# Two fused convolution layers: attention products paired in PSUM banks of their own, the limit on a softmax sum on GpSimd, the large quotients behind the small one

## The chip, the cores and the metric

The kernel runs on one core of a Trainium2 chip. The metric is the device time of one execution in microseconds; less is better. TensorE is called PE in the profile (PEld is its weight load), VectorE DVE, ScalarE ACT, GpSimd POOL, and SyncE, which issues most DMAs, SP.

## The reference, cut to what matters

```python
x = x + layer0(_gn(x), ...)   # 8 images of 256 channels, 64 x 64, all in float32
x = x + layer1(_gn(x), ...)

# layer 0, an involution
x1, x2, x3 = conv1x1(x, w1), conv1x1(x, w2), conv1x1(x, w3)     # 32, 32, 256 channels
h = relu(bn(concat([x1, unfold3(reflect_pad(x2))])))            # 32 * 10 channels
w = conv1x1(relu(bn(conv1x1(h, cw1))), cw2, cb2)                # 32 groups x 9 taps
out = sum_k unfold3(zero_pad(x3))[g, s, k] * w[g, k]            # g: 32 groups, s: 8

# layer 1, attention over 7 x 7 windows beside a dynamic convolution
att = softmax(q . (unfold7(k) + unfold7(pe)))                   # 4 heads of 64 channels, 49 keys
out_att = att . unfold7(v)
wts = softmax(conv1x1(x, Wfc).reshape(C, 9), over the 9)
hid = relu(dwconv(x, w1)); oc = dwconv(hid, w2)
out_conv = sum_9(oc * wts)                                      # = oc * sum(wts), as oc is the same for all 9
return rate1 * out_att + rate2 * out_conv
```

The kernel writes the last sum as a quotient: with eight exponentials taken relative to the ninth, the sum of the eight is `tot`, and the weight is tot / (tot + 1).

## The kernel before, in words

Each image is cut into 8 bands of 8 rows (512 positions). One loop runs over `g`, the bands of all images, starting 12 bands early: `g` is the band that layer 1 works on, and layer 0 works 10 to 12 bands ahead of it in the same loop. The first 12 rounds (`g < 0`, "alone") have layer 0 only; the last ones have layer 1 only. A round has 8 steps `s`: two channel halves `ct` of four steps `m`, and each step takes two 8 x 8 tiles of queries of the band.

The order of every engine's instructions is written out by hand (`tc.manual_schedule`): `advance()` moves a counter on, six times in a step, and `after(n, f)` puts work n moves later. Work with a place in the step goes into the lists `mid` and `end`, which `beside` fills. What an engine does is then in program order; the framework adds the semaphores, also for the rotation of buffers: a tile tag with n buffers hands them out in turn, and writing into a buffer waits for the last reader of the tile that had it n tiles ago.

What a step of layer 1 does, with the lines of the profile:

- PE: weighted values of an earlier step, 64 columns of the array wide (L747, 16 records, since a float32 product makes two); scores of this step, 64 x 64 (L703, 8); transposes of the last step's probabilities into `ptp` (L735, 4); the first `pf`, a 128 x 512 product for the dynamic weights (L825, 4); one product of the kind that the step has in `mid` (queries `pq` L637, keys `pk` L658, values `pv` L563, layer 0's `p3` L369, value transposes `pvt` L607); the second `pf`.
- DVE: masks the scores and takes their maximum (L712), adds weighted values to the output tile `xr` (L757), runs four taps of the depthwise convolutions (L782 and L808), takes the small reciprocal of the softmax sums (L727).
- ACT: exponentials of the scores (L720), scaling by the reciprocal (L729), copies `ptp` to `pt` (L737), exponentials of `pf` into `ex` (L830), and empties the other PSUM tiles.
- POOL: adds the `ex` of this step to that of the step before (L1026).

After the fourth step of a half, `dynamic_sum` adds the two halves of `ex` on POOL (L838); DVE adds 1 and limits (L845) and takes the quotient in two pieces, called large reciprocals below (L846, L850); POOL multiplies twice and adds to `xr` (L855, L856, L857, called the weighing below); SP stores `xr` (L862) after the second half.

Beside that runs layer 0 for later bands: `small_maps` makes `p12` (L328), from which ACT writes `x2` in eight pieces (L343, L347); `hidden_maps` scales it (L418) and makes `ph` (L429) and `h2n` (L435); `tap_weights` makes the nine taps' weights, three to a PSUM tile `pw` (L447), DVE multiplies each with the values (`prod`, L460, two buffers), POOL adds each product to `xg` (L468), and SP stores the result (L500).

[...] Before, `gen`, a tag of five, serves `ptp`, `pf`, `p12`, `ph`, `pw` and all `mid` products; the scores' tile `sco` takes two, and the weighted values lie in its free columns; `acc` of the depthwise convolutions takes one.

In SBUF, `ex` has three buffers, one for each step, and `rec`, the large reciprocal, one of its own. The end of `dynamic_sum`, which the change leaves as it is, and the lines that take an `ex` tile and free the one before:

```python
def weigh():
    engine.tensor_mul(tot, tot, rec)              # L855: tot is ex[:, 1] of the half's last step
    engine.tensor_mul(oc, oc, tot)                # L856: the last reader of that ex tile
    engine.tensor_add(xr[:, ct], xr[:, ct], oc)   # L857
    if ct == NCT - 1:
        after(6, store)
...
ex, exb = w1.tile([P, 2, BAND], F32, tag="ex", name=f"ex_{nm}", bufs=3), ex if m else None
branch_weights(b, i, ct, m, 0, ex)                # the first pf, L825, and its exponential, L830
...
after(4, lambda ex=ex, exb=exb: nc.gpsimd.tensor_add(ex, ex, exb))   # L1026, where there is an exb
```

Of the kernel before, what the change touches and what calls it, by code (L numbers as in the profile page):

```python
# [10 lines left out]
F32 = mybir.dt.float32  # L11
# [7 lines left out]
P = 128  # L19
# [20 lines left out]
TG = 3  # L40
# [25 lines left out]
TAPS_AT = (1, 3, 5), (0, 2, 4)  # L66
PRODUCTS_AT = ((1, 2, 7), (1, 2, 5), (1, 2, 7)), ((7, 14, 10), (9, 17, 13), (12, 20, 16))
# [19 lines left out]
def conv_layers_kernel(ctx: ExitStack, tc: tile.TileContext, ins: dict, out: bass.AP):  # L87
# [98 lines left out]
    def layer1_loads():  # L186


        last = w1.tile([P, NCT, 1, C], F32, tag="rec", name="last", bufs=1)
# [35 lines left out]
    def gn_affine(sts, means, name, done):  # L225
# [9 lines left out]
        def group_means(v, k):  # L235
            pg = ps.tile([P, n], F32, name=f"pg_{name}_{k}", tag="gen", bufs=5)
            nc.tensor.matmul(pg, means, v, start=True, stop=True)
            return pg
# [49 lines left out]
    def scaled_weights(b):  # L288
# [3 lines left out]
        def scale(sc, bi):  # L292
            im.w12s = w0.tile([P, NCT, 2 * REL], F32, tag="w12s", name=f"w12s_{b}", bufs=1)
            im.w3s = w0.tile([P, NCT, C], F32, tag="w3s", name=f"w3s_{b}", bufs=1)
            for kt in range(NCT):
                nc.vector.tensor_scalar(im.w12s[:, kt], w12[:, kt], sc[:, kt : kt + 1], None, ALU.mult)
                nc.vector.tensor_scalar(im.w3s[:, kt], w3[:, kt], sc[:, kt : kt + 1], None, ALU.mult)
            after(5, lambda: through(bi))

        def through(bi):  # L300
            pb = ps.tile([P, 1 + NCT], F32, tag="gen", name=f"pb_{b}", bufs=5)
# [18 lines left out]
    def small_maps(b, i):  # L320
# [4 lines left out]
        p12 = ps.tile([P, R // 2, W], F32, tag="gen", name=f"p12_{b}_{i}", bufs=5)  # L325
# [36 lines left out]
    def value_maps(b, i, mt):  # L362
# [4 lines left out]
        p3 = ps.tile([P, BAND], F32, tag="gen", name=f"p3_{b}_{i}_{mt}", bufs=5)  # L367
# [41 lines left out]
    def hidden_maps(b, i, at):  # L409
# [5 lines left out]
        def hidden(t):  # L415
            n = P if t == 0 else 96
            hid = w0.tile([P, R, W], F32, tag="hid", name=f"hid_{b}_{i}_{t}", bufs=2)
# [5 lines left out]
        def conv(first, last):  # L423
            if first == 0:
                im.ph = ps.tile([P, SR, W], F32, tag="gen", name=f"ph_{b}_{i}", bufs=5)
            for t in range(first, last):
                n = P if t == 0 else 96
                for q in range(NQR):
                    nc.tensor.matmul(  # L429
                        im.ph[q * REL : (q + 1) * REL], c1[:n, t], hids[t][:n, q * SR : (q + 1) * SR],  # L430
                        start=(t == 0), stop=(t == 2),
                    )

        def relu():
            nc.scalar.activation(h2n[i % 2][:, :, :W], im.ph, AF.Relu, bias=bn2b, scale=bn2s)  # L435

        hidden(0)
        for n, f in zip(at, (lambda: hidden(1), lambda: conv(0, 2), lambda: hidden(2), lambda: conv(2, 3), relu)):
            after(n, f)

    def tap_weights(b, i, u, alone, at):
# [3 lines left out]
        pw = ps.tile([P, TG, SR * HP], F32, tag="gen", name=f"pw_{b}_{i}_{u}", bufs=5)  # L445
        for j in range(TG):
# [55 lines left out]
        for j, n in enumerate(at):  # L502
            after(n, lambda j=j: product(j))
# [626 lines left out]
```

## Time and profile before

| | us |
|---|---|
| median of three runs | 4154.88 (4153.21 to 4155.15) |
| the profiled execution | 4152.64 |
| its span, first to last instruction | 4150.9 |
| start of the first scores / of band 54's / last scores | 246.3 / 3611.8 / 4131.5 |
| granted clock, mean | 0.993 |

A line of the page's group list gives line, engine, operation, output and inputs, shapes and count, then busy us and the mean ns of one. A line of a timeline gives start and duration in us, then the same, and in brackets how long the engine had been idle and what ended that. In a PE row the duration includes the last record's modelled end, so the time that a group takes is read from start to start. The table by stage gives for each stretch its length, then the busy us and count of PE, PEld, DVE, ACT, POOL, the clock, the DMA share and GB/s.

### The profile page before, as it was taken

The page shows a single profiled execution, that of the slowest core. Times are in us where ns is not written, and L with a number is a line of the kernel's source. Part 1 is how long each engine was busy: PE and PEld are TensorE (multiplying, and loading weights), DVE is VectorE, ACT ScalarE, POOL GpSimd, SP SyncE. Part 2 cuts the span into 40 slices and gives each one's busy share as a digit, 9 for nine tenths or more (in the row PEclk, how much of TensorE's full clock was granted, in tenths as well). Part 3 has the DMA queues.
Part 4 walks back from the last instruction along what each step waited for, and adds up shares of the span by engine and source line. Part 5 has one row for each costly group of instructions (what it writes and reads, how often), then busy time and mean ns, then how long its engine had stood idle before and what let it go on. Part 6 is the DMA issues. An engine that isn't in the chain of part 4 may idle for free.

```text
span 4150.9 us, 72735 instructions
## 1 busy us (share of the span) xinstructions
PE 4022.6 (97%) x25292; PEld 2126.8 (51%) x25292; DVE 3591.9 (87%) x7248; ACT 3081.0 (74%) x7726; POOL 2923.0 (70%) x1902
## 2 busy tenths in 40 slices
PE   6789999999999999999999999999999999999998
PEld 3345555555555555555555555555555555455554
DVE  5878998899898898889998898888988889977777
ACT  3467778777787777877778777777778777687776
POOL 4767777677786777777777777777777677744554
PEclk8999999999999999999999999999999999999999
DMA  8854234234244233334234234244233233111100
GB/s 226 194 135 111 73 91 109 72 94 109 62 101 107 76 94 98 81 94 109 72 85 118 72 94 105 66 101 106 71 82 99 65 87 85 33 41 39 39 28 21
DMA packets 381264, 367.89 MB, mean 89 GB/s; under 512 B 55648, under 2 KB 282720, under 8 KB 380640
## 3 DMA queue, kind: packets, MB, share of 16 engines
q1 hardware_dynamic: 377568, 358.68, 34.3%
q8 instruction: 200, 3.28, 0.3%
q10 hardware_dynamic: 3328, 4.55, 0.3%
q14 instruction: 168, 1.38, 0.1%
HBM read 261.42 MB, written 101.71 MB: 87 GB/s over the span
## 4 chain that ended last, share of the span: by engine, by line
PE 71%; DVE 14%; POOL 6%; ACT 5%; DMA 2%; issue 2%; SPq 1%; POOLq 0%; ACTq 0%; DVEq 0%
PE pf L825 33%; PE ptp L735 5%; PE sco L747 5%; PE pk L658 5%; PE sco L703 5%; PE p L369 5%; DVE prod L460 4%; PE pq L637 4%; POOL xg L468 3%; PE pvt L607 2%; PE pv L563 2%; DVE acc L808 2%; PE pw L447 2%; DVE acc L782 2%; POOL ex L1026 2%
## 5 line engine op out<-in xcount | busy, mean ns | idle before, releaser
L825 PE MATMUL pf<-yp,c_wfc 128*128 128x512 f32 x4096 | 1930.5, 595 | 10.6 <-ACT vc L581 5.0
L468 POOL TENSOR_TENSOR xg<-xg,prod 128x1024 f32<-128x1024 f32 x549 | 1203.9, 2193 | 96.6 <-DVE prod L460 64.1
L825 PEld LDWEIGHTS pf<-yp,c_wfc 128*128 128x128 f32 x4096 | 729.9, 190 | 690.5 <-issue 619.4
L1026 POOL TENSOR_TENSOR ex<-ex,ex 128x1024 f32<-128x1024 f32 x384 | 907.7, 2364 | 61.9 <-ACT ex L830 57.2
L830 ACT ACTIVATE ex<-pf 128x512 f32<-128x512 f32 x1024 | 607.3, 593 | 297.9 <-POOL ex L1026 141.3
L782 DVE SCALAR_TENSOR_TENSOR acc<-yp,c_chan,acc 128x504 f32<-128x504 f32 (+3 forms) x1104 | 766.2, 694 | 42.3 <-ACT acc L773 21.7
L460 DVE SCALAR_TENSOR_TENSOR prod<-pw,c_par,x3q 128x1040 f32<-128x1040 f32 x576 | 733.9, 1281 | 66.8 <-PE pw L447 21.6
L808 DVE SCALAR_TENSOR_TENSOR acc<-hid,c_chan,acc 128x504 f32<-128x504 f32 (+3 forms) x1024 | 757.8, 740 | 20.2 <-ACT acc L802 2.1
L855 POOL TENSOR_TENSOR ex<-ex,rec 128x512 f32<-128x512 f32 x127 | 162.3, 1278 | 809.5 <-DVE rec L850 767.1
L729 ACT ACTIVATE prob<-prob,tot 128x196 f32<-128x196 f32 x1024 | 411.6, 450 | 387.2 <-DVE tot L727 386.4
L712 DVE CUSTOM_DVE_ANT_0 prob<-sco,c_mask 128x196 f32<-128x196 f32 x1024 | 325.5, 355 | 272.4 <-PE sco L703 272.0
L720 ACT ACTIVATE prob<-prob,nmax 128x196 f32<-128x196 f32 x1024 | 461.4, 454 | 46.9 <-DVE nmax L712 45.3
L747 PEld LDWEIGHTS sco<-pt,vt 112*64 112x64 f32 x8160 | 283.8, 137 | 182.3 <-issue 51.7
L737 ACT COPY pt<-ptp 112x512 f32<-112x512 f32 x511 | 297.0, 581 | 105.0 <-PE ptp L735 103.0
L735 PE MATMUL ptp<-ident,prob 128*112 128x128 f32 x2044 | 341.7, 287 | 31.2 <-ACT prob L729 30.5
L747 PE MATMUL sco<-pt,vt 112*64 112x64 f32 x8160 | 347.0, 227 | 0.0
L735 PEld LDWEIGHTS ptp<-ident,prob 128*112 128x112 f32 x2044 | 203.9, 133 | 201.4 <-issue 77.7
L703 PE MATMUL sco<-kb,qb 64*64 64x196 f32 x4096 | 295.2, 357 | 0.0
L563 PE MATMUL pv<-yp,c_wv 128*128 128x512 f32 (+2 forms) x576 | 247.3, 554 | 0.6
L369 PE MATMUL p<-xc,w3s 128*128 128x512 f32 x512 | 244.4, 601 | 0.0
L658 PE MATMUL pk<-yp,c_wk 128*128 128x512 f32 (+2 forms) x576 | 240.8, 545 | 0.0
L637 PE MATMUL pq<-yp,c_wq 128*128 128x512 f32 x512 | 240.6, 592 | 0.0
(140 smaller groups left out, 5294.0 us busy)
## 6 DMA issues: line engine op xcount, KB each, us to landing
x<-x3n SPq DMA_DIRECT2D x128, 264.0 KB, 2.1
x3q<-x SPq DMA_DIRECT2D x128, 264.0 KB, 7.2
xc<-in_x SPq DMA_DIRECT2D x64, 512.0 KB, 5.0
xg<-in_x SPq DMA_DIRECT2D x256, 128.0 KB, 4.8
x<-xg SPq DMA_DIRECT2D x256, 128.0 KB, 2.4
yp<-x SPq DMA_DIRECT2D x128, 256.0 KB, 3.3
xr<-x SPq DMA_DIRECT2D x64, 512.0 KB, 5.8
out_x<-xr SPq DMA_DIRECT2D x64, 512.0 KB, 3.1
```

The source lines that it names most:

```text
L369: nc.tensor.matmul(p3, im.w3s[:, kt, mt * P : (mt + 1) * P], im.xc[i][:, kt, :], start=(kt == 0), stop=(kt == NCT - 1),)
L460: nc.vector.scalar_tensor_tensor(prod[:, :, :RUN], pw[:, j, :RUN].unsqueeze(1).to_broadcast([P, SHARE, RUN]), par[:, PCB2 + k : PCB2 + k + 1],
L468: nc.gpsimd.tensor_add(im.xg[i], im.xg[i], rows(prod))
L703: nc.tensor.matmul(sco[half[t], h, :NKEY], qb[half[h], 2 * m + t].rearrange("p r c -> p (r c)"), kb[half[h], :, c0 : c0 + KW], start=True, ...
L720: nc.scalar.activation(prob[:, h, :NKEY], prob[:, h, :NKEY], AF.Exp, bias=nmax[:, h : h + 1], scale=-1.0, accum_out=tot[:, h : h + 1],)
L735: nc.tensor.transpose(ptp[:, h, ch], prob[:, h, ch * CHUNK : (ch + 1) * CHUNK], ident)
L747: nc.tensor.matmul(po[half[h], :, t * TQ : (t + 1) * TQ], im.vt[i + ch, m][:n, t, (2 * ct + h) * HD : (2 * ct + h + 1) * HD], pt[:n, h, ch ...
L782: nc.vector.scalar_tensor_tensor(o, yp[:, ct, ra + dr : rb + dr, ca + dc : cb + dc], chan[:, ct, CW1 + k : CW1 + k + 1], o, ALU.mult, ALU.add,
L808: nc.vector.scalar_tensor_tensor(o, hid[:, ra + dr : rb + dr, ca + dc : cb + dc], chan[:, ct, CW2 + k : CW2 + k + 1], o, ALU.mult, ALU.add,)
L825: nc.tensor.matmul(pf, wfc[:, kt, 2 * m + j, ct * P : (ct + 1) * P], images[b].yp[i][:, kt, PAD : PAD + R], start=(kt == 0), stop=(kt == N ...
L830: nc.scalar.activation(ex[:, j].rearrange("p (r c) -> p r c", r=R), pf, AF.Exp)
L1026: after(4, lambda ex=ex, exb=exb: nc.gpsimd.tensor_add(ex, ex, exb))
```

## The change

- Scores are computed for two steps at once, at even steps, into the two banks of `sco` (columns 0 to 195 and 196 to 391 of each); the masking of each step stays in its step, as `masked`.
- The weighted values of two steps are computed together behind them, in a bank of their own (`small`), which also takes `p12` and `ph` when they are due. `gen` goes from five banks to four.
- The transposes of an odd step's probabilities stand behind the weighted values of the next even step; those of an even step stand behind the first `pf` of the odd step.
- The three products of `ph` become one group at step 6, with three `hid` buffers for two.
- Taps are made two to a `pw` tile at steps 1 to 5 (before: three at steps 1, 3 and 5), and their products follow 1 and 2 moves later.
- `dynamic_sum`'s "add 1 and limit" moves from DVE to POOL, right behind L838; the large reciprocals are taken 7 and 2 moves later instead of 5 and 3, which puts the first behind the small reciprocal of its step; they go into the half of `ex` that is free by then.
- The scaling of layer 0's weights moves from DVE to ACT.

```diff
-TAPS_AT = (1, 3, 5), (0, 2, 4)
-PRODUCTS_AT = ((1, 2, 7), (1, 2, 5), (1, 2, 7)), ((7, 14, 10), (9, 17, 13), (12, 20, 16))
+TAPS_AT = (1, 2, 3, 4, 5), (0, 2, 4)
+PRODUCTS_AT = ((1, 2),) * 5, ((7, 14, 10), (9, 17, 13), (12, 20, 16))
...
-                nc.vector.tensor_scalar(im.w12s[:, kt], w12[:, kt], sc[:, kt : kt + 1], None, ALU.mult)
+                nc.scalar.activation(im.w12s[:, kt], w12[:, kt], AF.Copy, scale=sc[:, kt : kt + 1])
...
-        p12 = ps.tile([P, R // 2, W], F32, tag="gen", name=f"p12_{b}_{i}", bufs=5)
+        p12 = home[:, 2 * P :].rearrange("p (r c) -> p r c", r=R // 2)
...
+    def score_of(sco, h, m):
+        return sco[:, h, m % 2 * NKEY : (m % 2 + 1) * NKEY]
...
-        ptp = ps.tile([CHUNK, 2, 2, P], F32, tag="gen", name=f"ptp_{nm}", bufs=5)
+        ptp = ps.tile([CHUNK, 2, 2, P], F32, tag="gen", name=f"ptp_{nm}", bufs=4)
...
+    def small_tile(nm):
+        return ps.tile([P, 4 * P], F32, tag="small", name=f"small_{nm}")
+
+    def weigh_steps(steps, home):
+        po = home[:, : 2 * P].rearrange("p (s r c) -> p s r c", s=2, r=R)
+        return [(a, weighted_values(*a, pt, po)) for a, pt in steps]
...
         engine.tensor_add(tot, tot, ex[:, 0])
-        rec = w1.tile([P, BAND], F32, tag="rec", name=f"rec_{b}_{i}_{ct}", bufs=1)
+        engine.tensor_scalar(tot, tot, 1.0, 1.0e37, ALU.add, ALU.min)
+        rec = ex[:, 0]
         n = BAND // 2
         def quotient():
-            nc.vector.tensor_scalar(tot, tot, 1.0, 1.0e37, ALU.add, ALU.min)
             nc.vector.reciprocal(rec[:, :n], tot[:, :n])
-            after(3, second)
+            after(2, second)
...
-        after(5, quotient)
+        after(7, quotient)
...
                 if g >= 0:
-                    sco = score_tile(nm)
-                    weighted = [(a, weighted_values(*a, pt, sco)) for a, pt in pending]
-                    prob, nmax = scores(b, i, ct, m, sco)
+                    weighted = []
+                    if m % 2 == 0:
+                        sco = score_tile(nm)
+                        for e in range(2):
+                            scores(b, i, ct, m + e, sco)
+                        small = small_tile(nm)
+                        weighted, pending = weigh_steps(pending, small), []
+                        if s == 0 and g + AHEAD < B * NB:
+                            mid.append(small_maps(*divmod(g + AHEAD, NB), small))
+                        if s == 6 and convs:
+                            convs.pop()(small)
+                        if before is not None:
+                            pending.append((before[:-1], transposed(nm, before[-1])))
+                    prob, nmax = masked(nm, m, sco)
                     for a, po in weighted:
                         add_values(*a, po)
-                    pending = [] if before is None else [(before[:-1], transposed(nm, before[-1]))]
                     tot = exponentials(nm, prob, nmax)
                 advance()
                 if g >= 0:
                     branch_weights(b, i, ct, m, 0, ex)
+                    if m % 2:
+                        pending.append((before[:-1], transposed(nm, before[-1])))
```

## Prediction, made before the changed kernel ran

> **What bounds the kernel now.** I read the page first, then busy time by stage, then the timelines of PE, ACT and GpSimd (POOL) over one band in the middle. The page says PE:
>
> ```profile
> PE 4022.6 (97%) x25292; PEld 2126.8 (51%) x25292; DVE 3591.9 (87%) x7248; ACT 3081.0 (74%) x7726; POOL 2923.0 (70%) x1902
> ```
>
> By stage (columns: us, then PE, PEld, DVE, ACT, POOL busy) PE is at 98.8% between the ramp and the tail, DVE at 90%, POOL at 75%:
>
> ```profile
> 1000.00:1500.00 500.00, 494.17 (x3152) 263.36 (x3151) 448.78 (x907) 385.92 (x968) 374.15 (x243) 1.00 0.37 91
> ```
>
> So PE's own order is the first limit, and a shorter PE band is worth something only until another engine's order binds. PE timeline, start and us, of step 1 of a band, then its steps 6 and 7:
>
> ```profile
> 2004.92 1.88 PE L369 MATMUL p<-xc,w3s 128*128 128x512 f32 x4
> 2006.73 0.69 PE L747 MATMUL sco<-pt,vt 112*64 112x64 f32 x16
> 2007.34 0.58 PE L703 MATMUL sco<-kb,qb 64*64 64x196 f32 x8
> 2007.85 0.65 PE L735 MATMUL ptp<-ident,prob 128*112 128x128 f32 x4
> 2008.34 1.88 PE L825 MATMUL pf<-yp,c_wfc 128*128 128x512 f32 x4
> 2010.06 0.60 PE L607 MATMUL pvt<-ident,vc 128*112 128x128 f32 x4
> ...
> 2052.53 0.57 PE L703 MATMUL sco<-kb,qb 64*64 64x196 f32 x8
> 2053.44 0.78 PE L735 MATMUL ptp<-ident,prob 128*112 128x128 f32 x4 [0.34 <-ACT prob L729]
> 2054.36 1.98 PE L825 MATMUL pf<-yp,c_wfc 128*128 128x512 f32 x4
> ```
>
> Start to start, a full 128x512 pair takes 1.72 us, but 1.81 ahead of a change to 64-column tiles; the small groups take 0.61 (L747), 0.51 (L703) and 0.49 (L735). The last rows show PE waiting in step 7 for scaled probabilities (0.91 and 0.92 in place of 0.51 and 0.49; in step 6 it loses 0.23 more). This band starts at 1999.49 (L747 of step 0), the next at 2061.06: 61.57 us, 1.06 of it these waits.
>
> GpSimd in that band, with the ACT row that waits for it:
>
> ```profile
> 2015.70 1.28 POOL L855 TENSOR_TENSOR ex<-ex,rec 128x512 f32<-128x512 f32 x1 [6.11 <-DVE rec L850]
> ...
> 2039.39 2.17 POOL L468 TENSOR_TENSOR xg<-xg,prod 128x1024 f32<-128x1024 f32 x1
> ...
> 2042.40 1.04 POOL L621 TENSOR_TENSOR pe<-pecol,perow 128x512 f32<-128x512 f32 x1
> 2048.31 1.28 POOL L855 TENSOR_TENSOR ex<-ex,rec 128x512 f32<-128x512 f32 x1 [4.86 <-DVE rec L850]
> 2049.67 1.27 POOL L856 TENSOR_TENSOR oc<-oc,ex 128x512 f32<-128x512 f32 x1
> ```
> ```profile
> 2050.97 0.60 ACT L830 ACTIVATE ex<-pf 128x512 f32<-128x512 f32 x1 [0.32 <-POOL oc L856]
> ```
>
> The reader is to see two things. GpSimd works without a gap from 2015.7 to 2043.4. And step 6's first exponential waits for L856: `ex` has three buffers, so step 6 takes step 3's, and L856 is its last reader. That wait is 0.32 us now.
>
> [...] the 0.32 wait above holds what stands behind it. [...] No row here has the added GpSimd tensor_scalar; a copy of 420 elements took 0.54, a two-input 512 op 1.27. I take 0.9, ends 0.5 and 1.3. [...]
>
> **The change part by part.** *Small products.* A 512-row pass is 0.43 us, so 64 rows are 0.054 and 196 rows 0.165. L747 streams 8 x 0.054 = 0.43 of its 0.61 (two column halves together), L703 2 x 0.165 = 0.33 of 0.51, L735 0.43 of 0.49. Two steps cost 2 x (0.09 + 0.61 + 0.51 + 0.49) = 3.40; together 0.09 + 0.84 + 1.04 + 0.49 + 0.43 = 2.89. Saved 0.5 a pair, 2.0 a band. The three hidden-layer products in one group instead of two save one entry and exit, 0.14. The transposes come later in their steps, and behind the small reciprocal the probabilities are ready earlier, so the 1.06 of waits go. PE alone would need 61.57 - 2.0 - 0.14 - 1.06 = 58.4 a band. From these groups its steps start at 0, 9.0, 15.5, 23.6, 29.6, 37.7, 43.6, 52.3.
>
> *DVE.* L845 leaves (137 us in 128), and 32 scalings of weights go to ACT (33 us of DVE; about 0.5 us each on ACT): off the path, as DVE is not full.
>
> *SP.* A half's output store follows its weighing, so it is issued some 5 us later, and the loads queued behind it (next bands' rows) with it; each has most of a band until it is used, so nothing. *Score bank.* It is rewritten every second step; DVE has masked its second half well before (step 5's at 42 for PE at 43.6): nothing.
>
> *Four shared banks for five.* p12 and ph leave the shared set, pw is held for two products instead of three; but bank k+4 now waits for k. Step 7's first pf waits for step 6's first pf.
>
> *GpSimd's order.* This is what I take as deciding. Before, six of nine `xg` sums stand ahead of the first half's L855. In the changed instruction order all nine do, and the tensor_scalar: products come at steps 1 to 5, two each, and the weighing moves from the end of step 5 into step 6, behind the ninth. Follow one band from its start:
> - ACT, step 0: the transposes of the last step end at 3.4; then copy 0.5, two exponentials 0.9, pf 0.5, scale 0.7, vt 0.5, eight x2 writes 3.85 (2005.52 to 2009.37), pf 0.55, x3n 0.6: 12.0. Step 1's exponentials end at 12.9.
> - DVE, step 1: the small reciprocal waits for them; it now stands ahead of the large ones, which before filled that wait. Then 0.13 + 1.67 + 1.45 (two taps) + 1.67 + product 0 at 1.2: 19.2.
> - GpSimd from 19.2: nine xg x 2.22 = 20.0, one weighing 3.94 (1.36 + 1.35 + 1.23), three L1026 x 2.3 = 6.9, kb 0.5, L838 1.25, tensor_scalar 0.9, pe 1.04, then L855 and L856 2.6: 37.1, so 56.3; with the ninth product, which DVE brings at 51.9 behind a reciprocal that waited for GpSimd, 56.7.
> - ACT's first exponential of step 6 then ends at 57.2 (before: 52). Queued behind it on ACT are h2n, the scaling, the queries and the second pf's exponential, for which PE waits in turn. It frees the bank of step 7's first pf, which PE would start at 52.3. From 57.2 step 7 takes 1.72 + 0.44 + 1.72 + 1.72 + 0.44 = 6.04: **63.2, against 61.57**.
>
> Had the transposes of step 7 a bank, they would wait for the scaling behind the same exponential (58.2), giving 62.5; a fifth bank alone would not cure it. The saved 2.0 us of PE lie beside this chain and are worth nothing in such a band.
>
> *Sum.* By the starts of step 0, the first 54 bands, which have layer-0 work, take 3365.5 us. In an image they take 68.8, 61.6, 61.6, 63.9, 61.6, 62.0, 59.3, 60.0. Band 0 has more PE and ACT work ahead of the chain: PE alone 65.6, chain 66.3, so -2.5. Bands 1, 2, 4: +1.6 each. Band 3, with the statistics: 0. Band 5, a memset more: +1.7. Bands 6 and 7, with less PE work but the same chain: +3.9 and +3.2. Together about +11 per eight, 54 x 1.36 = +74. The last ten bands (53.1) have no xg sums and save 2.0 each: -20. Ramp and tail: the conv's earlier relu and the weights on ACT gain or lose some 3 us: 0. Net +54 on the profiled execution's 4152.6 (span 4150.9): 4207; the three runs' median is 2.2 above that execution, inside the rounding. I say 4205.
>
> *Costs that the trace doesn't show.* The tensor_scalar on GpSimd: each 0.4 moves the chain 0.4, some 22 us in all. Merged groups: at worst no saving, still off the path here; at best 2.2. Four banks: nothing while the chain binds; else up to 1 us a band (in the trace, x3n and pv banks would be late by 0.2 to 1 us).
>
> **The rivals.**
> 1. *The chain binds, but starts earlier.* If product 0 came straight behind its bank (15.5 + 1.4 = 16.9) and the tensor_scalar took 0.5, L856 would end at 53.7 and the band at 60.4: ordinary bands -1.1, an average of about -1 over the image: -54 - 20, 4078. For it: DVE has 10% to spare. Against: ACT's 12.9 is a plain sum of rows.
> 2. *PE's floor.* If GpSimd keeps pace, each of 54 bands saves 3.2 less 0.5 for banks: -146 - 20, 3990. It needs L856 to end by 51.8, that is under 33 us of GpSimd work between product 0 and L856; the rows give 37. This is the point from which the sign turns: at 55.1 (T = 61.6) an ordinary band is even.
> 3. *A longer chain.* [...] the tensor_scalar takes over 1.3: +1.5 a band more, 4290.
> 4. *The merge does not stream back to back*: no gain on PE, which under the likeliest case changes only the last ten bands: 4225.
>
> **How the numbers follow.** The likeliest case with rival 4: 0.58, own range 4165 to 4260. Rival 3: 0.07. Rival 1: 0.17. Rival 2: 0.10. Cases that meet within 0.2% (8 us, about what a measurement of this kernel can tell from no change): 0.08. Slower 0.65, same 0.08, faster 0.27. The range 4065 to 4275 leaves out rival 2 and the outer parts of rivals 1 and 3, about 0.18.
>
> **What would show it.** Right: GpSimd without gaps from product 0 to the first weighing; ACT's `ex` exponentials waiting for POOL far longer than now (141.3 us for L1026, 24.5 for L856); PE idle ahead of the first pf or the transposes of step 7; L747's groups at 32 and L703's at 16, some 1.04 and 0.84 us long; bands of 63 us, the last ten 51. Wrong: PE still at 98% in the middle with bands near 58 to 60, or waits for POOL no longer than before.

## The result, and the profile after

The changed kernel takes 4301.93 us (4299.08 to 4304.44, four runs), the kernel before 4155.01 beside it: ratio 1.0354, 95% interval 1.0336 to 1.0372. It is slower by 147 us; the forecast was 4205, slower by 50, with a range that ended at 4275. Direction and mechanism hold, the size does not, and the range missed it.

The page's first part for the changed kernel, then its busy time by stage (columns as before):

```profile
PE 3985.3 (93%) x25292; PEld 2157.3 (50%) x25292; DVE 3433.3 (80%) x7089; ACT 3086.4 (72%) x7758; POOL 3152.3 (73%) x2029
```
```profile
1000.00:1500.00 500.00, 466.57 (x3040) 254.49 (x3039) 407.50 (x847) 367.71 (x929) 391.71 (x247) 0.99 0.36 89
```

PE is no longer full: 93.3% of the middle stage for 98.8%, and DVE 82% for 90%. Nobody is the bound by share; the bound is a chain across engines. The waits that belong to it, picked from the list of all waits (engine, its line, what it waited for: us in all, times, longest):

```profile
POOL xg L467 <- DVE prod L459: 497.7, 121, 10.1
ACT ex L842 <- POOL oc L868: 350.8, 117, 3.8
...
PEld pf L837 <- ACT ex L842: 218.2, 183, 3.9
PE pf L837 <- ACT ex L842: 150.2, 77, 3.7
...
DVE ex L858 <- POOL ex L853: 82.7, 54, 3.1
```

Most of the first is GpSimd's wait for the first product of each band (7.99 us in the band below); from that product on it works nearly without a gap. ACT's wait for the weighing (L868, L856 before) was 24.5 us and is 350.8, in two places of a band: behind the second half's weighing in step 2 and the first half's in step 6. L842 is the exponential of `pf` (L830 before), L853 the limit on GpSimd, L858 and L862 the large reciprocals, L867 to L869 the weighing. The end of one ordinary band, GpSimd, then ACT, then PE (the band starts at 2484.08, the next at 2548.69):

```profile
2529.04 1.92 POOL L853 TENSOR_SCALAR ex<-ex 128x512 f32<-128x512 f32 x1
...
2537.03 2.18 POOL L467 TENSOR_TENSOR xg<-xg,prod 128x1024 f32<-128x1024 f32 x1 [0.56 <-DVE prod L459]
2539.17 1.27 POOL L867 TENSOR_TENSOR ex<-ex 128x512 f32<-128x512 f32 x1
2540.52 1.26 POOL L868 TENSOR_TENSOR oc<-oc,ex 128x512 f32<-128x512 f32 x1
```
```profile
2541.81 0.60 ACT L842 ACTIVATE ex<-pf 128x512 f32<-128x512 f32 x1 [3.62 <-POOL oc L868]
```
```profile
2542.46 1.98 PE L837 MATMUL pf<-yp,c_wfc 128*128 128x512 f32 x4 [2.83 <-ACT ex L842]
```

This is the forecast chain, link by link: ninth sum, weighing, step 6's exponential, step 7's first `pf`, 6.23 us to the next band. Only the numbers are larger. Such a band takes 64.61 us; it was 61.57 and was forecast at 63.2.

Not all ordinary bands take 64.61: some take 66 to 68. The PE rows of one of those agree with the band above up to this one, which starts 58.4 us into both:

```profile
2015.80 3.78 PE L837 MATMUL pf<-yp,c_wfc 128*128 128x512 f32 x4 [2.87 <-ACT ex L842]
```

The same four records take 3.78 us, after nearly the same wait, and the two groups behind them are longer too. By stage around it, the column ahead of the last two is the granted clock:

```profile
2010.00:2014.00 4.00, 2.93 (x10) 1.24 (x8) 3.93 (x12) 0.99 (x4) 3.56 (x3) 1.00 0.03 8
2014.00:2018.00 4.00, 2.21 (x3) 1.17 (x4) 3.46 (x9) 2.86 (x7) 3.92 (x3) 0.64 0.54 123
2018.00:2022.00 4.00, 4.00 (x9) 1.80 (x8) 0.17 (x1) 3.09 (x9) 3.56 (x3) 0.50 0.00 0
2022.00:2026.00 4.00, 4.00 (x29) 1.99 (x29) 2.60 (x6) 0.91 (x2) 0.53 (x1) 1.00 0.08 10
```

While it waited, PE lost half its clock, and has it back 6.83 us later; in the band above, behind a wait of 2.83, it kept all of it. The clock records of this trace know two values, 1.0 and 0.5. Each of the 18 stretches at half clock in the first 54 bands lasts 3.41 or 6.83 us and starts a whole number of 3.413 us after the first one. "Lost clock" below is (1 - mean granted clock) times the length of the first 54 bands, from the trace's clock records: 41.0 us for the changed kernel, 3.8 before.

### The profile page after: what moved, and what is told of

The parts are those of the page before. It is cut to its first block, busy times and chain, and to the rows that moved or that the text cites. A ratio compares the mean times of both kernels' runs of the same rounds, so it can differ in the third digit from the quotient of the medians.

```text
span 4302.6 us, 72904 instructions
## 1 busy us (share of the span) xinstructions
PE 3985.3 (93%) x25292; PEld 2157.3 (50%) x25292; DVE 3433.3 (80%) x7089; ACT 3086.4 (72%) x7758; POOL 3152.3 (73%) x2029
## 4 chain that ended last, share of the span: by engine, by line
PE 46%; POOL 24%; DVE 13%; issue 9%; ACT 5%; DMA 2%; SPq 2%; POOLq 0%; DVEq 0%; ACTq 0%
PE pf L837 23%; POOL xg L467 9%; POOL ex L1055 5%; DVE prod L459 4%; PE small L750 3%; PE ptp L738 3%; POOL oc L868 3%; POOL ex L867 3%; PE pk L657 3%; PE pv L562 3%; PE sco L701 3%; DVE ex L858 3%; PE p L369 2%; DVE ex L862 2%; ACT ex L842 2%
## 5 line engine op out<-in xcount | busy, mean ns | idle before, releaser
L837 PE MATMUL pf<-yp,c_wfc 128*128 128x512 f32 x4096 | 1961.9, 603 | 164.8 <-ACT ex L842 150.2
L842 ACT ACTIVATE ex<-pf 128x512 f32<-128x512 f32 x1024 | 610.6, 596 | 648.0 <-POOL oc L868 350.8
L730 DVE RECIPROCAL tot<-tot 128x2 f32<-128x2 f32 x512 | 82.7, 161 | 334.2 <-ACT prob L723 331.9
L738 PE MATMUL ptp<-ident,prob 128*112 128x128 f32 x2044 | 324.9, 282 | 7.1 <-ACT vc L580 5.8
L738 PEld LDWEIGHTS ptp<-ident,prob 128*112 128x112 f32 x2044 | 230.7, 135 | 197.4 <-issue 106.6
L750 PEld LDWEIGHTS small<-pt,vt 112*64 112x64 f32 x8144 | 258.1, 137 | 76.0 <-issue 76.0
L750 PE MATMUL small<-pt,vt 112*64 112x64 f32 x8144 | 293.3, 225 | 0.0
L858 DVE RECIPROCAL ex<-ex 128x256 f32<-128x256 f32 x128 | 222.8, 1741 | 82.8 <-POOL ex L853 82.7
L867 POOL TENSOR_TENSOR ex<-ex 128x512 f32<-128x512 f32 x127 | 161.4, 1271 | 137.2 <-DVE ex L862 128.0
L657 PE MATMUL pk<-yp,c_wk 128*128 128x512 f32 (+2 forms) x576 | 251.5, 564 | 0.8
```

Source lines behind the costliest of these rows:

```text
L657: nc.tensor.matmul(pk[:, :n], wk[:, kt, ct * P : (ct + 1) * P], im.yp[i][:, kt, a : a + n], start=(kt == 0), stop=(kt == NCT - 1),)
L738: nc.tensor.transpose(ptp[:, h, ch], prob[:, h, ch * CHUNK : (ch + 1) * CHUNK], ident)
L750: nc.tensor.matmul(po[half[h], :, t * TQ : (t + 1) * TQ], im.vt[i + ch, m][:n, t, (2 * ct + h) * HD : (2 * ct + h + 1) * HD], pt[:n, h, ch ...
L837: nc.tensor.matmul(pf, wfc[:, kt, 2 * m + j, ct * P : (ct + 1) * P], images[b].yp[i][:, kt, PAD : PAD + R], start=(kt == 0), stop=(kt == N ...
L842: nc.scalar.activation(ex[:, j].rearrange("p (r c) -> p r c", r=R), pf, AF.Exp)
```

## Experiments

Ordinary band: mean of bands 1, 2 and 4 of the second to the sixth image, from the profiled execution. The medians are of four to six executions (more of the kernel before); the ratio is to the kernel before, run on the same chip. "Into the band" counts from the band's first scores.

| run | us, median | ratio, 95% | ordinary band | lost clock |
|---|---|---|---|---|
| before | 4155.0 | 1 | 61.57 | 3.8 |
| changed | 4301.9 | 1.0354 (1.0336-1.0372) | 65.45 | 41.0 |
| e1 limit on DVE | 4361.0 | 1.0492 (1.0474-1.0509) | 66.85 | 66.6 |
| e2 quotients back | 4298.1 | 1.0338 (1.0323-1.0354) | 64.35 | 70.0 |
| e3 both back | 4310.3 | 1.0371 (1.0355-1.0386) | 64.85 | 75.1 |
| e4 four `ex` | 4144.7 | 0.9969 (0.9958-0.9981) | 61.95 | 10.2 |
| e5 taps by three | 4355.5 | 1.0472 (1.0455-1.0490) | 66.93 | 105.8 |
| e6 pairs only | 4397.8 | 1.0577 (1.0561-1.0592) | 66.78 | 104.1 |
| e7 no limit | 4193.0 | 1.0085 (1.0070-1.0100) | 63.11 | 0.0 |
| e8 four `ex`, taps by three | 4198.0 | 1.0088 (1.0065-1.0111) | 63.71 | 41.0 |
| e9 filler, small bank | 4568.4 | 1.0993 (1.0975-1.1011) | 70.71 | 52.9 |
| e10 four `ex`, no limit | 4077.2 | 0.9813 (0.9798-0.9827) | 60.23 | 5.1 |
| e11 before + limit on GpSimd | 4130.6 | 0.9941 (0.9926-0.9956) | 60.90 | 1.7 |
| e12 before, four banks | 4241.4 | 1.0207 (1.0192-1.0222) | 62.84 | 11.9 |
| e13 filler, score bank | 4337.1 | 1.0435 (1.0417-1.0452) | 65.06 | 3.4 |
| e14 before + late quotients | 4353.0 | 1.0474 (1.0459-1.0490) | 65.02 | 90.4 |
| e15 four `ex`, other limit | 4199.3 | 1.0104 (1.0089-1.0119) | 63.34 | 5.1 |
| e17 e11 + four `ex` | 4130.9 | 0.9936 (0.9923-0.9950) | 60.89 | 3.6 |
| e18 limit at 0.9 us | 4221.5 | 1.0164 (1.0147-1.0181) | 63.73 | 3.4 |

### Is `ex` the link? (e4)

```diff
-        oc = w1.tile([P, BAND], F32, tag="oc", name=f"oc_{b}_{i}_{ct}")
+        oc = w1.tile([P, BAND], F32, tag="oc", name=f"oc_{b}_{i}_{ct}", bufs=1)
...
-                    ex, exb = w1.tile([P, 2, BAND], F32, tag="ex", name=f"ex_{nm}", bufs=3), ex if m else None
+                    ex, exb = w1.tile([P, 2, BAND], F32, tag="ex", name=f"ex_{nm}", bufs=4), ex if m else None
```

> The changed kernel with four ex buffers for three (space from oc, one buffer for two). GpSimd's order and the limit stay. Theory (ex is the link by which the weighing holds PE): step 6 takes the tile of step 2, so only step 7's first exponential waits for the weighing, about 7 us later in the band; the weighing still ends near 57.7 and that exponential near 58.4, by when PE has three of step 7's products behind it: bands 59.5 to 61.5, time 4040 to 4140. Rival (GpSimd's and DVE's own pace sets the band, by the products and their buffers): bands 63.5 to 64.6, time 4240 to 4302.

4144.7: 157 us faster than the changed kernel, and 0.3% faster than the kernel before, with GpSimd's order untouched (L868 still ends 57.7 us into the band). PE's two longest waits of step 7 are what is left of the 2.83:

```profile
2563.51 1.99 PE L837 MATMUL pf<-yp,c_wfc 128*128 128x512 f32 x4 [0.27 <-ACT ex L842]
2565.74 0.65 PE L738 MATMUL ptp<-ident,prob 128*112 128x128 f32 x4 [0.25 <-ACT qb L640]
```

The weighing ends as late as in the changed kernel, and 157 us are gone: it costs them through the `ex` tile that it holds. That is shown. The band of 61.95 is 0.45 above the expected window, the time 5 us; PE's floor of 58.4 is not reached even so.

### The limit (e1, e7, e10, e11, e15, e16)

e1 moves it back to DVE:

```diff
-engine.tensor_scalar(tot, tot, 1.0, 1.0e37, ALU.add, ALU.min)
...
 def quotient():
+    nc.vector.tensor_scalar(tot, tot, 1.0, 1.0e37, ALU.add, ALU.min)
     nc.vector.reciprocal(rec[:, :n], tot[:, :n])
```

> The changed kernel with "add 1 and limit" back on DVE, in front of the first large reciprocal. Theory (GpSimd's chain from the first product to the first half's weighing sets the band): the chain loses the tensor_scalar, 1.92 + 0.07 us, and gains back some tenths because DVE's 0.42 us stands in front of the reciprocals. Ordinary bands 62.6 to 63.1 for 64.6; time 4195 to 4225 for 4302; ACT's wait for the weighing shrinks by about 1.5 us in step 6. Rival (the place of the weighing behind the ninth product alone does it, and the ninth product comes late from DVE in any case): bands stay above 64, time above 4280.

Slower by 59, not faster by 90. DVE in step 5 of a band:

```profile
2565.45 0.16 DVE L730 RECIPROCAL tot<-tot 128x2 f32<-128x2 f32 x1
2565.53 1.89 DVE L857 TENSOR_SCALAR ex<-ex 128x512 f32<-128x512 f32 x1
2567.45 1.75 DVE L858 RECIPROCAL ex<-ex 128x256 f32<-128x256 f32 x1
```

GpSimd is busy there with `xg`, and the row takes 1.89 us, where the same row in step 1, with GpSimd idle, takes 0.41. The first reciprocal starts 47.8 us into the band for 46.9, and the ninth product, the sum behind it and the band (65.48 where the clock holds, for 64.61) all move by the same 0.9. So the way to the ninth product runs over DVE as well as over GpSimd, the limit sits on it from either engine, and with the stretched row on DVE it is 0.9 longer. The theory that GpSimd's work alone makes the chain falls.

e7 leaves the limit out:

> The changed kernel without "add 1 and limit" (that operation is left out on every engine; quotient and weighing stay). It prices the GpSimd tensor_scalar by its absence. Theory A: the large reciprocal then waits only for DVE's own order (45.5 for 46.9), so the ninth product and the weighing come 1.4 us earlier, not 1.9; ordinary bands 63.2, time 4220 to 4240. Rival (GpSimd alone is the chain, each us on it counts in full): 62.6, time 4190 to 4205. Rival 2 (DVE binds without it): above 4280.

Both numbers came true, one from each side: the band is 63.11, as theory A had it (the reciprocal starts at 45.4 in DVE's own order), but the time fell by 109. The 1.5 us a band are 80 us in 54 bands; PE's wait in step 7 fell from 2.83 to 1.33 and the lost clock from 41 to nothing:

```profile
2593.22 1.98 PE L837 MATMUL pf<-yp,c_wfc 128*128 128x512 f32 x4 [1.33 <-ACT ex L842]
```

e10 leaves it out of e4, e11 gives it to GpSimd in the kernel before:

> Four ex buffers and no "add 1 and limit" at all (left out on every engine). With three buffers leaving it out took 109 us off. Theory (its price is paid only through the weighing's hold on the ex tile and so on PE): with four buffers it has cover; between 4125 and 4146, at most 20 us below the run with four buffers. Rival (GpSimd's and DVE's own pace sets the band in any case): 80 to 110 us below, 4035 to 4065.

> The kernel before with one edit: "add 1 and limit" moved to GpSimd behind the addition of the two halves. GpSimd waits 5.5 to 6 us ahead of each weighing there, so 1.9 us more has cover, and DVE loses a row that took 2.37 us in step 5 while GpSimd was busy (median 0.42). Theory: 4140 to 4165, no change that matters. Rival (the tensor_scalar costs its 1.9 us per half wherever it stands): 4200 to 4260.

e10 is 67 us below e4: with four buffers the price falls from 109 to 67, not to 20. What is left does not go through `ex`: DVE's first large reciprocal waits 2.70 us for the limit in e4, and in e10 0.73 for the addition ahead of it (46.9 and 45.0 us into the band). Step 6's masks stand behind it on DVE, ACT's exponentials of the scores behind those, and PE's two waits of step 7 that e4 shows are not there in e10. e11 is a gain of 25 us: GpSimd waited 5.6 us ahead of the first half's weighing in the kernel before, and hides 1.92 there. DVE at the same place, in the kernel before and in e11:

```profile
2412.72 2.37 DVE L845 TENSOR_SCALAR ex<-ex 128x512 f32<-128x512 f32 x1 [0.41 <-POOL ex L838]
2415.13 1.75 DVE L846 RECIPROCAL rec<-ex 128x256 f32<-128x256 f32 x1
```
```profile
2522.88 1.75 DVE L846 RECIPROCAL rec<-ex 128x256 f32<-128x256 f32 x1 [2.19 <-POOL ex L839]
```

The reciprocal starts 41.8 us into the band before and 41.2 in e11, and the ordinary band is 0.67 shorter. So the limit is better placed on GpSimd in both kernels: by 25 us here, and by the 59 of e1 in the changed one. The 109 us of e7 are the price of the operation itself there, where neither engine hides it.

e15 tries another form on DVE, in e4 (`most` is a column of 1e37):

```diff
-engine.tensor_scalar(tot, tot, 1.0, 1.0e37, ALU.add, ALU.min)
...
+nc.vector.scalar_tensor_tensor(tot, tot, 1.0, most.to_broadcast([P, BAND]), ALU.add, ALU.min)
```

> Four ex buffers, and "add 1 and limit" on DVE in front of the first large reciprocal as a scalar_tensor_tensor (add 1, minimum with a column of 1e37), a form whose rows of 504 columns take 0.75 us here whether GpSimd is busy or not. Theory: the reciprocal starts about 1.3 us earlier than with the limit on GpSimd (45.6 for 46.9), nearly as with no limit; bands 60.3 to 60.9; time 4075 to 4105. Rival (DVE's added 0.75 us per half costs as much as the limit on GpSimd did): 4135 to 4160.

The rival is right, and worse: 4199, 55 above e4. The form is held up too: its row takes 2.66 us in step 5, with GpSimd at work, and 0.67 in step 1, with GpSimd idle, as the other form's took 1.89 and 0.41 in e1. The taps' rows do not stretch: the same operation with one input in PSUM takes 0.66 to 0.75 us for 504 columns in the kernel before, with GpSimd idle or at work. The row of step 5:

```profile
2586.46 2.66 DVE L859 SCALAR_TENSOR_TENSOR ex<-ex,most 128x512 f32<-128x512 f32 x1 [0.68 <-POOL ex L852]
```

e16 measures four GpSimd forms, four times each, ahead of the bands of the changed kernel (one execution, 4298.1 us):

> The changed kernel with four GpSimd forms on 128x512 float32, four times each, ahead of the bands: tensor_scalar with add and min, tensor_scalar with add alone, copy, two-input add. Theory (each of the two operations is a pass of its own): 1.92, about 0.96, about 0.6, 1.27. Rival (a tensor_scalar costs 1.9 us whatever it does): 1.92, 1.9, 0.6, 1.27.

```profile
L1006 POOL TENSOR_SCALAR trial<-trial 128x512 f32<-128x512 f32 x4 | 7.7, 1921 | 0.3
L1007 POOL TENSOR_SCALAR trial<-trial 128x512 f32<-128x512 f32 x4 | 6.0, 1492 | 0.3
L1009 POOL TENSOR_TENSOR trial<-trial 128x512 f32<-128x512 f32 x4 | 5.1, 1271 | 0.3
L1008 POOL COPY trial<-trial 128x512 f32<-128x512 f32 x4 | 2.4, 609 | 0.3
```

Neither theory: one operation costs 1.49, the second adds 0.43. A one-input tensor_scalar with one operation is dearer here than an addition of two inputs (1.49 and 1.27).

### Where the quotients stand (e2, e3, e14)

e2 puts `after(5, quotient)` and `after(3, second)` back, e3 also the limit:

> The changed kernel with the large reciprocals back in front of the small one (5 and 3 moves for 7 and 2); the limit stays on GpSimd. In GpSimd's order the weighing of the second half then stands in front of the first product and that of the first half in front of the ninth. Theory: the chain loses one weighing (3.94 us), which GpSimd does while it waits for the first product, and one sum (2.2 us), less 0.6 by which the earlier weighing can delay the first sum: first weighing ends near 52, PE's floor (58.4) plus the waits for scaled probabilities (about 1 us) becomes the bound: bands 59.5 to 61, time 4040 to 4110. Rival (DVE's order: with the large reciprocals in front, probabilities come so late that PE loses what the chain gives): bands above 62.5, time above 4190.

> Both edits to the end of dynamic_sum undone (limit on DVE, large reciprocals in their old place); the paired products, the taps by twos, the four shared banks and the weights' scaling on ACT stay. Theory: the chain ends 2 us earlier still than with the quotients alone put back, but PE's own order is the bound by then: bands 59 to 60.5, time 4030 to 4090, at most 40 us under the run with the quotients back. Rival (four shared banks, not the chain, cost the time): bands above 63, time above 4220.

No gain: 4298 and 4310. The weighing does end earlier (its second product at 54.6 us for 57.7), but DVE pays for it, as e2's rival said. DVE in e2:

```profile
2648.52 1.75 DVE L858 RECIPROCAL ex<-ex 128x256 f32<-128x256 f32 x1 [3.13 <-POOL ex L853]
2660.14 0.61 DVE L769 SCALAR_TENSOR_TENSOR xr<-small,bv,xr 128x128 f32<-128x128 f32 x2 [2.40 <-POOL xr L869]
```

The first wait now stands in front of step 5's small reciprocal, so ACT stands idle for 5.9 us ahead of scaling step 5's probabilities, and PE's transposes wait 1.5 us. The second is new: the pairs of step 6 are added to `xr` just when the weighing writes it. e3 holds DVE up at the same two places (there the limit's own row, 2.38 us, stands in front of the small reciprocal), so its loss is no proof for its rival, the banks. Both lose some 30 us of clock more than the changed kernel, which is in these times.

e14 makes only the quotients late, in the kernel before:

```diff
-            after(3, second)
+            after(2, second)
...
-        after(5, quotient)
+        after(7, quotient)
```

> The kernel before with the large reciprocals 7 and 2 moves later for 5 and 3 (behind the small one of their step); nothing else. Theory (the prediction's mechanism: a later weighing holds the ex tile that step 6 needs): DVE's limit stands behind the small reciprocal, the weighing comes 3 to 5 us later, ACT's first exponential of step 6, which waits 0.3 us now, waits 3 to 5; bands 63 to 66, time 4240 to 4380. Rival (GpSimd has the slack of 5.5 us ahead of the weighing, so nothing follows): 4140 to 4170.

4353, slower by 198, with five banks and nothing paired. GpSimd ahead of the first half's weighing, and ACT in step 6:

```profile
2690.20 2.19 POOL L468 TENSOR_TENSOR xg<-xg,prod 128x1024 f32<-128x1024 f32 x1 [4.41 <-DVE prod L460]
2692.34 1.27 POOL L855 TENSOR_TENSOR ex<-ex,rec 128x512 f32<-128x512 f32 x1
2693.69 1.27 POOL L856 TENSOR_TENSOR oc<-oc,ex 128x512 f32<-128x512 f32 x1
```
```profile
2694.99 0.60 ACT L830 ACTIVATE ex<-pf 128x512 f32<-128x512 f32 x1 [3.57 <-POOL oc L856]
```

GpSimd is not short of time here (it waits 4.4 us for DVE); the weighing is late because DVE's reciprocals, and the product behind them, are. But these waits of step 6, which the expectation named, cost PE nothing: from the start of step 4 to the end of the band it takes 31.3 us for 31.4 before. An ordinary band's loss is all in step 3, 11.6 us for 8.1, and comes from the other half's weighing, which now stands in step 2:

```profile
2662.57 0.60 ACT L830 ACTIVATE ex<-pf 128x512 f32<-128x512 f32 x1 [3.16 <-POOL oc L856]
```
```profile
2663.56 0.92 PE L735 MATMUL ptp<-ident,prob 128*112 128x128 f32 x4 [1.61 <-ACT prob L729]
2664.27 3.48 PE L825 MATMUL pf<-yp,c_wfc 128*128 128x512 f32 x4
```

The link is the forecast one (the weighing holds an `ex` tile, ACT's exponential waits for it, the scaled probabilities queue behind), but in a place that the prediction did not follow, and about half of the price is the clock (90.4 of the 198 us): the `pf` group takes 3.48 us, for 1.88 in the next one.

### Taps, pairs and banks (e5, e6, e8, e12)

```diff
-TG = 2, 3
-TAPS_AT = (1, 2, 3, 4, 5), (0, 2, 4)
-PRODUCTS_AT = ((1, 2),) * 5, ...
+TG = 3, 3
+TAPS_AT = (1, 3, 5), (0, 2, 4)
+PRODUCTS_AT = ((1, 2, 7), (1, 2, 5), (1, 2, 7)), ...
```

> The changed kernel with the taps by threes again (three to a pw tile at steps 1, 3 and 5, products 1, 2 and 7 or 5 moves later); limit on GpSimd and late quotients stay. Then five sums stand ahead of the first half's addition L850 in GpSimd's order, not six, and seven of nine ahead of the weighing. Theory A (the band is set by the chain GpSimd's sums, L850, limit L853, DVE's first large reciprocal, its next product, its sum, the weighing): L853 ends 2.2 us earlier, the reciprocal starts near 44.7 for 46.9, the weighing ends near 55.5 for 57.7; ordinary bands 62.2 to 63.2; time 4170 to 4225. Theory B (only the number of sums ahead of the weighing counts, as the prediction had it: two fewer): 4.4 us less, PE the bound, time below 4120. Rival (taps by twos are not at fault): above 4280.

> Both edits to the end of dynamic_sum undone and the taps by threes: what stays of the change is the pairing of the small products in a bank of their own, four shared banks, the transposes' new places, the weights' scaling on ACT. GpSimd's order is then that of the kernel before. Theory A: L850 ends near 39.5 for 42.3 in the run with only the first two undone, the large reciprocals no longer hold the small one of step 5, and PE's 1.9 us of waiting for probabilities in step 6 goes; bands 60 to 62.5, time 4070 to 4160. Rival (pairing itself or the fourth bank loses): bands above 63, time above 4220.

> Four ex buffers and the taps by threes together, the limit on GpSimd and the late quotients kept: a candidate for a kernel that beats both. Theory A: with the weighing no longer the link, what holds PE at 61.9 in the run with four ex buffers is some 3.5 us of short waits (keys from DVE ahead of step 4's scores, queries and exponentials from ACT in step 7); an earlier large reciprocal relieves those behind DVE: bands 60.5 to 61.9, time 4070 to 4145. Rival (those waits come from ACT's and PE's own order): no change from four buffers alone, 4135 to 4155.

Each loses: 54 us on the changed kernel (e5), 88 on e3 (e6), 53 on e4 (e8, which lies above both of its expectations). In e5 GpSimd did what theory A said (the reciprocal starts at 45.2, the weighing's second product ends at 55.9 for 57.7), yet PE waits for banks sooner: 2.4 us at `pvt`, 1.0 at `pf`, and the `pf` behind them takes 3.78 us. In e6 one wait of PE is 4 us long:

```profile
2723.71 2.45 PE L837 MATMUL pf<-yp,c_wfc 128*128 128x512 f32 x4 [3.97 <-ACT qb L640]
```

ACT empties the queries' bank so late because its queue stands behind step 6's probabilities, and those behind DVE. Taps by twos are a gain in the paired kernel, though they put one more sum ahead of the limit: the prediction counted only what they cost. How much of the three losses is the bank waits and how much the clock behind them stays open: lost clock rises by 65, 29 and 31 us with them.

e12 takes one bank from the kernel before (`bufs=5` to `bufs=4` for `gen`) and gives it to nobody:

> The kernel before with four gen banks for five, nothing else (one bank stays empty). It prices the bank that the pairing takes, though p12 and ph still come from gen here. Theory (the bank is a main part of what pairing loses, since the run with pairs only lost 243 us): PE waits for banks that ACT and DVE free late, bands 64 to 68, time 4280 to 4420. Rival (the prediction's: up to 1 us a band, so the loss of the paired kernels lies in the order of small products and probabilities): below 4215.

86 us, 1.3 in an ordinary band, 3 in the first of an image. PE waits 0.90 for ACT's `x2` writes (L347) in step 1 and 0.76 for value windows (L581) in step 6. This lies between the two expectations, nearer to the rival's.

### The lost clock (e9, e13, e18)

e9 and e13 put matmuls that nobody reads into PE's wait of step 7:

```diff
+if s == 7 and g + AHEAD - 1 < B * NB:
+    for _ in range(REPS):        # REPS is 20; in e13 16, into sco[:, 0, 2 * NKEY :], ahead of masked()
+        nc.tensor.matmul(small[:, 3 * P :], ident, wfc[:, 0, 0, :P], start=True, stop=True)
```

> The changed kernel with 20 matmuls of 128 columns into unused columns of the small bank, ahead of step 7's first pf (2.1 us of PE work whose result nobody reads), in the first 53 bands. It fills most of the 2.9 us that PE waits there, and adds nothing to the result. Theory (the wait costs twice: the time itself, and in some bands a stretch at half clock behind it, which the records show as pf groups of 3.78 us for 1.98): the stretches at half clock between bands 0 and 53, 41 us of lost clock, shrink to under 10; the bands of 66 to 68 us fall to 64.6; time 4262 to 4280. Rival (the slow groups have another cause and the clock follows them): no fewer of them, time 4300 to 4330, more by what the filler pushes back.

> The changed kernel with 16 matmuls of 120 columns into the unused columns of the score bank, ahead of step 7's first pf in bands 0 to 52 (1.6 us of PE work that nobody reads; in this place only step 6's masking, done long before, stands in their way). They fill more than half of the 2.9 us that PE waits there. Theory (the wait makes TensorE lose its clock in part of the bands): lost clock in the first 54 bands 41 us -> under 10, no pf group of 3.78 us, bands of 66 to 68 us gone, time 4265 to 4285. Rival (slow groups have another cause): 4295 to 4330.

e9 does not test it: the tile that it writes also holds `ph`, which ACT reads behind the very exponential that PE waits for, so the filler came after the wait (124.4 us of PE's waits are for that row) and not into it. e13 settles the clock and misses the time. Lost clock falls from 41.0 to 3.4 us, no `pf` group takes 3.78 us, ordinary bands of 66 to 68 are gone. But 32 records took 3.57 us, not 1.6 (0.11 each, with a weight load for each), so ordinary bands are 65.06, 0.45 above the undisturbed 64.61, and bands 3, 6 and 7 pay 2.5, 2.3 and 3.6 for work in a place where PE waited less.

e18 gives GpSimd a cheaper operation in the limit's place; it leaves out the addition of 1 and the limit:

```diff
-engine.tensor_scalar(tot, tot, 1.0, 1.0e37, ALU.add, ALU.min)
+most = ex.rearrange("p t n -> p (t n)")[:, 144:]
+engine.tensor_copy(most, most)
```

> The changed kernel with "add 1 and limit" replaced by an in-place GpSimd copy of 880 columns of the ex tile (the addition and the limit are left out): by the rows of 420 columns (0.54 us) and 512 (0.61) an estimated 0.9 us, the duration that the prediction took. It stands in the same chain: behind L850, ahead of the first large reciprocal. Theory (one mis-sized term, with the loss of clock as its consequence): the reciprocal waits 0.4 us for 1.4, PE waits under 2 us in step 7 and keeps its clock; ordinary bands 63.5 to 63.8, lost clock in the first 54 bands under 10 us, time 4200 to 4225, the predicted 4205 within 0.5%. Rival (the loss of clock and the rest have other causes): clock loss of 30 us or more stays, time 4235 to 4260.

```profile
L854 POOL COPY ex<-ex 128x880 f32<-128x880 f32 x127 | 116.5, 918 | 8.1
```
```profile
2599.24 1.75 DVE L859 RECIPROCAL ex<-ex 128x256 f32<-128x256 f32 x1 [0.41 <-POOL ex L854]
```

With 0.918 us in that place everything falls where theory had it: the reciprocal waits 0.41 for 1.40, the undisturbed band is 63.6, lost clock 3.4, and the time 4221.5, 0.4% above the forecast of 4205. (The bands' own errors in the forecast partly cancel in that sum, as listed below.)

### A version that beats both (e17)

> The kernel before with "add 1 and limit" on GpSimd (as e11) and four ex buffers (the large reciprocal written into the free half of ex, one oc buffer for two make the room). Theory: ACT's waits of 1.2 and 2.0 us for the additions of ex and 0.3 for the weighing go; PE's own order of unpaired products is the bound at about 60.5 for 60.9: 0.2 to 0.5 us a band, time 4100 to 4125. Rival (those waits have cover in PE's order): 4126 to 4135, no change from 4131.

The rival: 4130.9, no change from e11 (4130.6). Where the weighing is early, a fourth `ex` tile has nothing to free. The best kernel with nothing left out is therefore the kernel before with one edit, the limit on GpSimd: 0.6% faster than before, 4% faster than the changed one.

## Why the prediction was wrong in size, and right in kind

- **PE's groups**: right. L701 takes 0.85 for 16 records, L750 1.08, L738 0.49 and 0.44, as forecast (0.84, 1.04, 0.49, 0.43).
- **PE's floor of 58.4**: never reached, 60.23 at best (e10). Step starts of e4 are 0, 8.9, 16.2, 24.2, 31.4, 39.4, 45.3, 54.7 for a forecast of 0, 9.0, 15.5, 23.6, 29.6, 37.7, 43.6, 52.3: DVE's keys ahead of step 4's scores (0.95) and ACT's order had no term.
- **The chain's start**: right. ACT's exponentials of step 1 end at 12.9, product 0 at 18.9 (forecast 19.2). But the terms that the forecast lists up to 12.0 add up to 11.5; the trace has the 12.0, with a wait of 0.30 us of ACT for PE among its rows that no term names. So 12.9 is not the plain sum of rows that the prediction holds against rival 1.
- **The chain's length**: the step that failed. The term "tensor_scalar 0.9" measures 1.92, outside the ends of 0.5 and 1.3. It acts as the prediction's own side remark had it, through "a reciprocal that waited for GpSimd": that wait is 1.40, so the ninth product, the weighing (57.7 for 56.7) and the band move by 1.0. The rest of an undisturbed band's 1.4 is 0.2 in the hand-over and 0.2 in step 7 (6.23 for 6.04). The signs named for a right mechanism came: GpSimd with one gap of 0.56 us from product 0 to the weighing, ACT waiting for POOL, PE idle ahead of step 7's first `pf`.
- **A term that was not there**: the clock. In the changed kernel PE's clock fell by half during or just behind 12 of the 27 waits of 2.8 to 2.9 us, and the lost clock is 41.0 us for 3.8.
- **The size of the two together**: the first 54 bands were to take 74 us more and took 167. In e18, with the 0.9 that the sum had used, they take 3446.7 us, 81 more than before and 7 from the forecast. So 86 of the 93 us are the mis-sized duration and the lost clock behind it, and e13 shows that the clock's part hangs on that wait. How the 86 divide is only estimated: 1.0 us in each of 54 bands is 54, which leaves some 32 for the clock.
- **Bands**: the first of an image was to gain 2.5 and lost 1.6; at 68.4 in e18 it is 2.1 above its forecast even with the right duration. Bands 6 and 7 came out as forecast (63.0 and 63.7 for 63.2), but by luck: with the forecast's duration, in e18, they take 62.0 and 62.6. The last ten save 1.8 each for 2.0 (51.3 for 53.1 in most of them); from the start of band 54 to the end it is -17.5 for -20, and the ramp is +2 for 0.
- **Four banks**: "up to 1 us a band" is 1.6 in the kernel before (86 us over 54 bands). In the changed kernel it was not tried alone.
- **Limit's "DVE leaves, off the path"**: wrong. Its place in step 5 (2.37 us) was worth 25 us in the kernel before, and e1 puts 59 on it in the changed one.
- **Rival 3** (a longer chain, 4290) was the case that came; it got 0.07. The 0.9 and its ends were the author's estimate, set between a copy of 420 elements (0.54) and a two-input addition of 512 (1.27), neither of which is this form: a tensor_scalar on GpSimd takes 1.49 with one operation and 1.92 with two (e16). The measurement decides.

What the runs do not give is one edit to blame. From the kernel before, late quotients alone cost 198 us, pairs with four banks and the transposes' new places 243; the taps by twos take 88 of that back, and the whole change stands at 147. The costs do not add, and no run shows how they overlap.

One sentence ahead of the prediction is wrong: L845 writes tot + 1 back into `tot`, so the quotient is (tot + 1) / (tot + 1), the sum of all nine weights. No duration depends on it.

## What to carry to other kernels

Before work moves to another engine, ask for a row of exactly that form on that engine; where there is none, its bounds are wide, and a chain that runs through it carries the width into every round. Ask next which buffer the moved work holds and who waits for that buffer: here one more `ex` tile was worth 157 us, and none where the reader was early. And price a wait of TensorE of a few us above its length, since the clock can go with it: here 16 of the 18 stretches at half clock set in at waits of 2.35 to 2.9 us, and all 18 together cost 41 us.

## What the hardware did that was not expected

- GpSimd, 128x512 float32 (e16): tensor_scalar with two operations 1.92 us, with one 1.49, two-input add 1.27, copy 0.61. On DVE the two-operation form takes 0.41 to 0.43 in the kernel before where GpSimd is idle, and up to 2.86 while GpSimd works; a scalar_tensor_tensor with its column in SBUF 0.67 with GpSimd idle, and 2.66 while GpSimd works (e15).
- In the first 54 bands of the changed kernel half clock set in during, or within 1.3 us after, 12 of 27 waits of PE between 2.8 and 2.9 us and 4 of 7 waits of 2.35. The length of the single wait does not decide: 15 of those 27 left the clock full, and in e14 a wait of 1.61 us in step 3 has a `pf` group of 3.48 us behind it. The 90.4 us that e14 lost are as much as 53 stretches of 3.41 us at half clock, in 54 bands.
- How busy PE was around the wait tells more. With the trace of the changed kernel cut into pieces of 3.413 us, on the grid on which its half-clock stretches start, PE's matmul rows fill 16 to 42% of the 18 pieces ahead of a stretch and 42% or more of the 992 pieces after which the clock stayed full. In the kernel before they fill 45 and 48% of the two pieces ahead of a stretch and 54% or more of the others. These are two traces, and they put the border in different places: what sets the clock is not shown by them.
